# A four-layer stack on one core: rotary partners side by side, norms in tiles of 64 tokens, and another written order

## The chip, the core and the metric

The kernel runs on one core of a Trainium2 chip. The metric is the time of one execution on the device in microseconds, as the median over runs. A core has five engines that work side by side, each through its own queue of instructions in order: TensorE (matrix products, PE in the profile, its weight loads PEld), VectorE (DVE), ScalarE (ACT), GpSimd (POOL) and SyncE (SP), which issues nearly all transfers here. Products land in PSUM, a small memory of 8 banks that TensorE alone fills and that VectorE and ScalarE empty. All else lies in SBUF, 128 partitions of one row each.

## What is computed

The input is 16 sequences of 256 tokens with 128 features. Four blocks follow one another: causal attention with 16 small heads; a feed-forward part with a choice of two experts in eight; a retention layer; and at last a stack of six layers, each with local attention and a feed-forward part. The change lies in the stack's attention. Cut to what matters:

```python
def attn_layer(x, Wqkv, qs, ksc, Wo):          # 16 heads of 64, windows of 32
    q, k, v = heads(x @ Wqkv)
    q, k = l2norm(q) * qs, l2norm(k) * ksc
    q = q * cos * scale + rotate_half(q) * sin * scale
    k = k * cos / scale + rotate_half(k) * sin / scale
    out = local_attention(q, k, v)             # own window and the one before, causal, softmax
    return out @ Wo
for i in range(6):
    x = attn_layer(shift_tokens(x), ...) + x
    x = ffn_layer(shift_tokens(x), ...) + x
```

`rotate_half` exchanges the two halves of a head's 64 features and turns one's sign: feature f and feature f + 32 are rotary partners. All is in float32.

## The kernel before

**Units.** In the stack the kernel works with features on partitions and tokens along the row. A unit is one sequence in one layer's attention; 6 layers by 16 sequences give 96 units, two of them (a pair of sequences) sharing one feed-forward part. A unit has four head groups G. Two partition halves by two slots (`hf`) make four heads of 64 features in each group; q and k are the index k. The methods of `Unit` are its steps, named in the order by short words:

- `pqk` (L925): projection of group G, q or k, into one PSUM bank; two banks take turns (`ps_qk`). `sq` (L933, ScalarE), `t2` (L942) and `rot` (L947, both VectorE) read it: the squares, the product with the sines and the product with the cosines, the last one into the tile `qk`, of which there are eight (two units).
- `sw` (L958, SP): the partners' products change places, by transfers from `t` to `t2s`. `add` (L964, GpSimd) adds them to `qk`.
- `nr` (L973): sums of squares of each head and token, by products with `gather`, a matrix of zeros and ones that also sets the row in which each sum lands. 8 tiles of 32 tokens by 2 slots by 4 groups, in two words `nr.0` and `nr.1`. `rnA` (L985), `rnB` (L988), `rnC` (L991): max, square root, reciprocal.
- `bcW` (L997) sends the reciprocals to DRAM (`ndr`, two in turn), `bcR` (L1006) reads those of a group back, spread over 64 partitions at a time, into `bc` (one tile for each group). `norm` (L1013, GpSimd) multiplies `qk` by them.
- `s` (L1042): scores, in PSUM tiles shared with `o` (two in turn). `sm`, `mx`, `sub`, `exp`, `su`, `rec`, `nm`, `tp` (L1058 to L1098): band, maximum, subtraction (GpSimd), exponential (ScalarE), sum, reciprocal, multiplication (GpSimd), transposition, for each slot `hu`.
- `xt`, `xc` (L1021, L1029): the tokens transposed as values. `o` (L1112), `oTc` (L1125), `y` (L1131), `xsu` (L1141): weighted sums, their copy, the output product (value and output weights multiplied ahead), and the residual.
- `fn` to `xsf` (L1157 to L1261) in `Forward`: the feed-forward part of a pair.

`nr`, `xt`, `y` and the feed-forward products share two PSUM banks in turn (`ps_m`).

**Order.** `ORDER` (L1278) is written out by hand or by a planner beforehand: a list of words `step.arguments:distance`. One round of the loop runs the whole list once for two units; the distance says which unit a word belongs to, counted from the round's first. So words of a dozen units, early projections and late feed-forward steps, alternate, and each engine's queue is what the list has for it. Nothing is reordered later. `BRIDGE`, another such list, leads from the retention layer into the stack; `FIRST` orders the blocks before it.

Of the kernel before, what the change touches and what calls it, by code (L numbers as in the profile page):

```python
# [28 lines left out]
DEPTH, H2, D2, WIN = 6, 16, 64, 32  # L29
INNER = H2 * D2  # L30
# [8 lines left out]
def _tables():  # L39

    c = {}
    c["ident"] = np.eye(P)
    i = np.arange(P)
    diag = np.where(i[None, :] > i[:, None], NEG, 0.0)
    c["mask0"] = np.concatenate([diag, np.zeros((P, P)), diag], 1)

    qi = i[:, None] % WIN  # L50
    key = np.arange(WIN)[None, :]
    band = np.concatenate([key >= qi, key <= qi], 1)
    first = band & ((i[:, None] >= WIN) | (np.arange(2 * WIN)[None, :] >= WIN))
    band = np.where(np.stack([first, band], 1), 0.0, NEG)
    c["band"] = np.repeat(band[:, :, None, :], 4, 2).reshape(P, 512)


    t = np.arange(T, dtype=np.float64)
    inv = 1.0 / 10000.0 ** (np.arange(0, DK1, 2) / DK1)
    f = np.outer(t, inv)  # L60
    cs = np.concatenate([np.cos(f), np.cos(f)], 1)
    sn = np.concatenate([-np.sin(f), np.sin(f)], 1)
# [12 lines left out]

    half = np.arange(0, D2, 2, dtype=np.float64)
    f = (1.0 / 10000.0 ** (half / D2))[:, None] * t[None, :]
    base = (half + 0.4 * D2) / (1.4 * D2)  # L80
    sc = base[:, None] ** ((t - T // 2) / (WIN // 2))[None, :]
    both = np.stack([8.0 * sc, 1.0 / sc])
    cos = np.stack([np.cos(f) * both, np.cos(f) * both], 1)
    sin = np.stack([np.sin(f) * both, -np.sin(f) * both], 1)
    tabs = np.stack([cos, sin]).transpose(2, 3, 0, 1, 4).reshape(D2, -1)
    c["rot2"] = np.tile(tabs, (2, 1))


    e = np.arange(WIN)
    sb = np.arange(16)  # L90
    gather = (i[:, None, None] // D2 == e[None, None, :] // 16) & (e[None, None, :] % 16 == sb[None, :, None])
    c["gather"] = gather.reshape(P, -1)


    e = np.arange(NE)
    sel = (np.arange(NE * RANK)[None, :] // RANK) == e[:, None]
    c["expand"] = np.concatenate([sel, np.zeros((P - NE, NE * RANK))])
    before = (e[None, :] < e[:, None]).astype(np.float64).reshape(1, -1)
    c["before"] = np.broadcast_to(before, (P, NE * NE))
    return {k: np.ascontiguousarray(v, dtype=np.float32) for k, v in c.items()}  # L100
# [7 lines left out]
def kernel(ctx: ExitStack, tc: tile.TileContext, a: dict, widths: dict, out: bass.AP):  # L108
    nc = tc.nc
# [6 lines left out]
    dram = ctx.enter_context(tc.tile_pool(name="dram", bufs=1, space=bass.MemoryType.DRAM))  # L116
# [13 lines left out]
    c = {}  # L130
# [576 lines left out]
    for g in range(NPAIR):  # L707
        xt = xres.tile([P, 2, XW], F32, name=f"xs{g}")
# [84 lines left out]
    for n in range(2):  # L793
        t = ea.tile([P, 2, 4, 4, 32], F32, name=f"less{n}")
# [49 lines left out]
    s2 = ctx.enter_context(tc.tile_pool(name="s2", bufs=2, **right))  # L844
# [5 lines left out]
    for n in range(NRING):  # L850
        t = lw.tile([P, 2, 2, WIN + T], F32, name=f"qk{n}")
        nc.gpsimd.memset(t[:, :, :, 0:WIN], 0.0)
        ring.append(t)
    band = c["band"]
    gather = c["gather"].rearrange("p (s b m) -> p s b m", s=2, b=8)

    ndr = [dram.tile([2, H2, T], F32, name=f"ndr{n}") for n in range(2)]
    def load_qk(l, G):

        w = lw.tile([P, 2, 2, P], F32, tag=f"wqk{G}", name=f"wqk{l}_{G}")  # L860
        src = a["wqk2"][l].rearrange("d (g k h n) -> d g k h n", g=4, k=2, h=2)
        nc.sync.dma_start(out=w, in_=src[:, G])
        return w
# [40 lines left out]
    class Unit:  # L904
# [48 lines left out]

        def sw(self, G):

            for to in range(4):
                at = to ^ 1
                nc.sync.dma_start(  # L958
                    out=self.t_2s(G)[32 * to : 32 * to + 32], in_=self.t_2(G)[32 * at : 32 * at + 32]
                )  # L960

        def add(self, G):
            to = self.qk_t[G][:, :, :, WIN : WIN + T]
# [2 lines left out]


        def nr(self, part):
            nr = self.misc("nr")[:, 0:64]
            for b in range(4 * part, 4 * part + 4):  # L970
                for slot in range(2):
                    for G in range(4):
                        nc.tensor.matmul(  # L973
                            nr[32 * G : 32 * G + 32, :],
                            lhsT=gather[:, slot, b, :],
                            rhs=self.squares(G)[:, :, slot, WIN * b : WIN * b + WIN],
                            start=(b == 0 and slot == 0),
                            stop=(b == 7 and slot == 1),
                        )

        def r_n(self):
            return self.tile(s2, [P, 64], "rn")

        def rnA(self):
            nc.vector.tensor_scalar(self.r_n(), self.misc("nr")[:, 0:64], 1e-24, None, ALU.max)  # L985

        def rnB(self):
            nc.scalar.activation(self.r_n(), self.r_n(), AF.Sqrt)  # L988
# [2 lines left out]
            nc.vector.reciprocal(self.r_n(), self.r_n())  # L991

        def bcast(self, G):
            return self.tile(s2, [P, 2, 2, T], "bc", G, tag=f"bc{G}", bufs=1)

        def bcW(self):
            nc.sync.dma_start(  # L997
                out=ndr[self.u % 2].rearrange("k h (b t) -> (h b) k t", t=WIN),
                in_=self.r_n().rearrange("p (k t) -> p k t", k=2),
            )  # L1000

        def bcR(self, G):

            for r in range(2):
                at = 4 * G + 2 * r
                nc.sync.dma_start(  # L1006
                    out=self.bcast(G)[64 * r : 64 * r + 64].rearrange("p k s t -> p k (s t)"),
                    in_=ndr[self.u % 2][:, at : at + 2].rearrange("k s t -> k (s t)").partition_broadcast(64),
                )

        def norm(self, G):
            to = self.qk_t[G][:, :, :, WIN : WIN + T]
            nc.gpsimd.tensor_tensor(to, to, self.bcast(G), ALU.mult)  # L1013


        def xt(self):
# [126 lines left out]
    class Forward(Unit):  # L1143
# [132 lines left out]


    ORDER = """  # L1278
        rnB:0 rs:-4 rot.3.1:0 t2.1.1:1 pqk.1.0:1 fg.2:-6 oTc.1.0:-2 sq.1.0:1 s.1.1.1:-1 sw.3:0 s.1.0.0:-1 rnC:0
        s.1.1.0:-1 t2.1.0:1 s.1.0.1:-1 oTc.1.1:-2 y.0:-2 bcW:0 sq.1.1:1 rot.1.0:1 rot.1.1:1 pqk.0.1:1 sw.1:1 y.1:-2  # L1280
        pqk.0.0:1 sm.1:-1 exp.0:-1 mx.1:-1 y.2:-2 t2.0.1:1 add.3:0 su.0:-1 rot.0.1:1 z:-4 sq.0.1:1 sub.1:-1 sq.0.0:1
        exp.1:-1 t2.0.0:1 rot.0.0:1 pqk.3.1:1 bcR.2:0 add.1:1 bcR.0:0 rec.0:-1 pqk.3.0:1 y.3:-2 sq.3.0:1 nm.0:-1
        su.1:-1 rec.1:-1 bcR.1:0 sq.3.1:1 rot.3.1:1 t2.3.1:1 nm.1:-1 bcR.3:0 norm.0:0 t2.3.0:1 sw.0:1 gl.2:-6 pqk.2.0:1
        rot.3.0:1 sq.2.0:1 pqk.2.1:1 fa.2:-6 tp.0:-1 xsu:-2 tp.1:-1 add.0:1 sq.2.1:1 nr.0:1 o.1:-1 nr.1:1 fh.2:-6
        trf:-4 oTc.1.0:-1 norm.1:0 rot.2.1:1 oTc.1.1:-1 norm.3:0 rot.2.0:1 t2.2.1:1 t2.2.0:1 pqk.1.1:2 rnA:1 xt:0 rnB:1
        rnC:1 sw.3:1 fz:-4 sw.2:1 o.0:-1 pqk.1.0:2 bcW:1 oTc.0.0:-1 norm.2:0 xc:0 bcR.3:1 fg.0:-4 s.0.1.0:0 add.3:1
        sq.1.1:2 t2.1.0:2 s.0.0.0:0 sq.1.0:2 s.0.0.1:0 oTc.0.1:-1 gl.0:-4 s.0.1.1:0 sm.0:0 fy:-6 bcR.2:1 fa.0:-4 mx.0:0
        t2.1.1:2 s.1.1.1:0 add.2:1 s.1.0.1:0 s.1.0.0:0 xsf:-6 s.1.1.0:0 sub.0:0 rot.1.1:2 sm.1:0 y.0:-1 pqk.0.0:2
        y.1:-1 mx.1:0 rot.1.0:2 pqk.0.1:2 exp.0:0 t2.0.0:2 rot.0.0:2 su.0:0 sq.0.0:2 norm.3:1 t2.0.1:2 sq.0.1:2
        pqk.2.1:2 bcR.0:1 norm.2:1 sub.1:0 sw.1:2 rot.0.1:2 exp.1:0 y.2:-1 bcR.1:1 sq.2.1:2 rec.0:0 fh.0:-4 pqk.2.0:2  # L1290
        y.3:-1 sw.0:2 rot.2.1:2 t2.2.1:2 pqk.3.0:2 fg.1:-4 s.0.0.1:1 norm.0:1 sq.2.0:2 su.1:0 norm.1:1 rec.1:0 gl.1:-4
        s.0.1.1:1 s.0.1.0:1 nm.0:0 rot.2.0:2 xsu:-1 s.0.0.0:1 t2.2.0:2 nm.1:0 fn:-2 tp.0:0 sm.0:1 pqk.3.1:2 nat:-2 xt:1
        tp.1:0 fa.1:-4 t2.3.0:2 xc:1 sq.3.1:2 o.0:0 sq.3.0:2 oTc.0.0:0 add.1:2 mx.0:1 t2.3.1:2 nr.0:2 rot.3.0:2 sw.2:2
        oTc.0.1:0 add.0:2 pqk.1.1:3 st:-2 add.2:2 fh.1:-4 sub.0:1 nr.1:2 o.1:0 rnA:2
    """.split()


# [156 lines left out]
```

## Time and profile before

| what | value |
| --- | --- |
| median of 3 runs | 3719.79 us (3716.75 to 3724.08) |
| the profiled execution's own time | 3729.29 us |
| its span, from first to last instruction | 3727.5 us |
| TensorE busy | 3369.8 us (90%) |
| GpSimd busy | 2855.7 us (77%) |
| VectorE busy | 2656.2 us (71%) |
| ScalarE busy | 2021.2 us (54%) |
| transfers | 459.58 MB, mean 123 GB/s |
| swap transfers (`t2s<-t`) | 1536 of 128 KB |
| norm reads (`bc<-ndr`) | 768 of 256 KB |

The profile comes from one execution. Its page gives each engine's busy time, the same in 40 equal slices of the span, the chain of work that ended last (followed back from the end, at each step to what released it), and groups of equal instructions with their mean time and the idle time of the engine ahead of them. A wait is written as "engine tile line <- what ended it", with the total, the number of times and the longest. SPq is SP's queue, busy while it issues a transfer. A matrix product in float32 leaves two records. Views of the trace show the same for any stretch of time.

### The profile page before, as it was taken

What the parts mean: (1) busy time and instruction counts of PE and PEld (TensorE: products, weight loads), DVE (VectorE), ACT (ScalarE), POOL (GpSimd) and SP (SyncE); (2) the same over time, 40 slices, a digit from 0 to 9 for tenths busy, and PEclk for the clock granted to TensorE, in tenths of its full rate; (3) what the DMA queues carried; (4) which work ended last, traced back from release to release, by engine and by line L of the source; (5) the groups of instructions that cost most, each with busy time, mean ns of one, the idle gap of its engine ahead of it and who ended that gap; (6) DMA issues with size and microseconds to landing.
All of it is one profiled execution on the core that took longest, in us unless ns stands there. A gap on an engine that the chain in (4) does not pass through costs nothing.

```text
span 3727.5 us, 124065 instructions
## 1 busy us (share of the span) xinstructions
PE 3369.8 (90%) x53280; PEld 2360.1 (63%) x53280; DVE 2656.2 (71%) x5196; ACT 2021.2 (54%) x2933; POOL 2855.7 (77%) x1753
## 2 busy tenths in 40 slices
PE   5999986699999999999999999999999999999997
PEld 3666665466666666666666666666666666666664
DVE  4667664577777777777786777777777777777773
ACT  2455543355656555556555565555565655555552
POOL 2445445688888888888888888888988898888882
PEclk7999998799999999999999999999999999999999
DMA  3111103566665656565656666656566666656561
GB/s 94 27 38 33 41 15 95 132 145 149 136 156 121 161 137 158 124 158 123 166 128 148 140 139 143 151 134 153 134 143 150 143 140 152 136 135 143 130 150 31
DMA packets 245698, 459.58 MB, mean 123 GB/s; under 512 B 66462, under 2 KB 85020, under 8 KB 245020
## 3 DMA queue, kind: packets, MB, share of 16 engines
q1 hardware_dynamic: 244716, 451.38, 52.0%
q8 instruction: 419, 6.86, 0.9%
q14 instruction: 131, 1.07, 0.1%
q10 hardware_dynamic: 432, 0.26, 0.0%
HBM read 235.47 MB, written 14.68 MB: 67 GB/s over the span
## 4 chain that ended last, share of the span: by engine, by line
PE 29%; DMA 20%; DVE 17%; POOL 14%; SPq 9%; issue 7%; ACT 3%; POOLq 0%; DVEq 0%; ACTq 0%
DMA t2s<-t 10%; DMA bc<-ndr 7%; SPq L958 5%; PE o L1112 5%; POOL qk L964 5%; POOL qk L1013 5%; PE pqk L925 4%; DVE t L942 4%; SPq L1006 4%; DVE qk L947 3%; DVE pT L1098 3%; PE s L1042 2%; PE nr L973 2%; PE p L327 2%; PE fy L1246 2%
## 5 line engine op out<-in xcount | busy, mean ns | idle before, releaser
L964 POOL TENSOR_TENSOR qk<-qk,t2s 128x1024 f32<-128x1024 f32 x384 | 904.5, 2367 | 305.1 <-DMA t2s<-t 272.8
L925 PE MATMUL pqk<-xs,wqk 128*128 128x256 f32 x3072 | 831.6, 394 | 107.2 <-DVE t L942 44.5
L1013 POOL TENSOR_TENSOR qk<-qk,bc 128x1024 f32<-128x1024 f32 x384 | 899.7, 2364 | 34.1 <-DMA bc<-ndr 26.7
L933 ACT ACTIVATE sq<-pqk 128x512 f32<-128x512 f32 x768 | 445.2, 600 | 588.9 <-DVE qk L947 310.9
L925 PEld LDWEIGHTS pqk<-xs,wqk 128*128 128x128 f32 x3072 | 554.6, 192 | 320.1 <-PE pqk L925 64.8
L942 DVE TENSOR_TENSOR t<-pqk,rot 128x512 f32<-128x512 f32 x768 | 515.5, 682 | 334.4 <-PE pqk L925 145.8
L1131 PE MATMUL y<-oT,m 128*128 128x256 f32 x3072 | 739.3, 384 | 11.6 <-issue 7.6
L1131 PEld LDWEIGHTS y<-oT,m 128*128 128x128 f32 x3072 | 577.9, 191 | 97.6 <-issue 9.6
L947 DVE TENSOR_TENSOR qk<-pqk,rot 128x512 f32<-128x512 f32 x768 | 514.7, 680 | 152.8 <-ACT sq L933 77.0
L1125 ACT COPY oT<-o 128x1024 f32<-128x1024 f32 x384 | 380.7, 1018 | 356.1 <-PE o L1112 356.1
L1073 POOL TENSOR_TENSOR sm<-sm,mx 128x1024 f32<-128x1024 f32 x192 | 365.7, 1905 | 87.5 <-DVE mx L1069 72.2
L1112 PE MATMUL o<-pT,xv 32*128 32x512 f32 x3072 | 395.0, 627 | 33.7 <-DVE pT L1098 28.4
L1042 PEld LDWEIGHTS s<-qk 64*32 64x32 f32 x24576 | 265.1, 105 | 218.2 <-POOL qk L1013 69.1
L1091 POOL TENSOR_TENSOR sm<-sm,rec 128x1024 f32<-128x1024 f32 x192 | 361.7, 1904 | 33.8 <-DVE rec L1087 33.3
L1042 PE MATMUL s<-qk 64*32 64x64 f32 x24576 | 309.4, 226 | 61.1 <-POOL qk L1013 41.6
L1058 DVE TENSOR_TENSOR sm<-s,c_band 128x1024 f32<-128x1024 f32 x192 | 234.2, 1220 | 151.6 <-PE s L1042 146.4
L973 PEld LDWEIGHTS nr<-sq,c_band 128*32 128x32 f32 x12288 | 185.2, 111 | 160.5 <-issue 93.4
L1077 ACT ACTIVATE sm<-sm 128x1024 f32<-128x1024 f32 x192 | 202.8, 1056 | 153.1 <-POOL sm L1073 149.2
L1112 PEld LDWEIGHTS o<-pT,xv 32*128 32x128 f32 x3072 | 142.3, 188 | 185.3 <-issue 100.3
L1098 DVE STREAM_TRANSPOSE pT<-sm 128x1024 f32<-128x1024 f32 x192 | 237.6, 1237 | 19.1 <-POOL sm L1091 17.6
L1222 ACT ACT_TABLE_LOAD x138 | 177.1, 1283 | 133.1 <-PE fg L1216 125.4
L973 PE MATMUL nr<-sq,c_band 128*32 128x64 f32 x12288 | 220.1, 222 | 30.2 <-issue 29.0
(191 smaller groups left out, 4444.1 us busy)
## 6 DMA issues: line engine op xcount, KB each, us to landing
t2s<-t SPq DMA_DIRECT2D x1536, 128.0 KB
bc<-ndr SPq DMA_DIRECT2D x768, 256.0 KB
wqk<-in_wqk_dram SPq DMA_DIRECT2D x24, 256.0 KB
rot_l<-in_rot_dram SPq DMA_DIRECT2D x12, 256.0 KB
rot<-rot_l SPq DMA_DIRECT2D x12, 256.0 KB
rot<-rot SPq DMA_DIRECT2D x6, 512.0 KB
ndr<-rn SPq DMA_DIRECT2D x96, 32.0 KB
wv<-in_wv_dram SPq DMA_DIRECT2D x6, 512.0 KB
```

What stands on the lines that cost most here:

```text
L925: nc.tensor.matmul(self.p_qk(G, k)[:, hf, :], lhsT=weights["qk", G, self.l][:, k, hf, :], rhs=xq, start=True, stop=True)
L933: nc.scalar.activation(self.squares(G)[:, k], self.p_qk(G, k), AF.Square)
L942: nc.vector.tensor_tensor(self.t_2(G)[:, k], self.p_qk(G, k), self.turn(1, k), ALU.mult)
L947: nc.vector.tensor_tensor(self.qk_t[G][:, k, :, WIN : WIN + T], self.p_qk(G, k), self.turn(0, k), ALU.mult)
L964: nc.gpsimd.tensor_tensor(to, to, self.t_2s(G), ALU.add)
L973: nc.tensor.matmul(nr[32 * G : 32 * G + 32, :], lhsT=gather[:, slot, b, :], rhs=self.squares(G)[:, :, slot, WIN * b : WIN * b + WIN], star ...
L1013: nc.gpsimd.tensor_tensor(to, to, self.bcast(G), ALU.mult)
L1042: nc.tensor.matmul(ps[32 * b : 32 * b + 32, r2, tt, G // 2, G % 2, :], lhsT=qk[G][rows, 0, hu, WIN + at : 2 * WIN + at], rhs=qk[G][rows, 1 ...
L1073: nc.gpsimd.tensor_tensor(s3, s3, self.t_mx(hu)[:, :, None].to_broadcast([P, 16, 2 * WIN]), ALU.subtract)
L1112: nc.tensor.matmul(self.p_o(tt, b // 2)[:, b % 2].rearrange("f (h g) q -> f h g q", g=4), lhsT=self.t_xv()[rows, n, tt, :], rhs=pT[rows, : ...
L1125: nc.scalar.copy(self.t_oT()[:, :, at : at + 2 * WIN].rearrange("f h (b q) -> f b h q", b=2), self.p_o(tt, c))
L1131: nc.tensor.matmul(self.misc("y")[:, 0:T], lhsT=weights["m", self.l][:, h, :], rhs=self.t_oT()[:, h, :], start=(h == 0), stop=(h == H2 - 1),)
```

## The change

Three things are changed in the stack.

1. **Rotary partners on neighbouring partitions.** The columns of the projection weights are permuted on the host, and the cosine, sine and scale tables with them, so that features f and f + 32 of a head lie on partitions 2f and 2f + 1 of its half. The swap then exchanges even and odd partitions: two transfers of 64 rows, each taking every second partition, where there were four of 32 neighbouring rows.
2. **Norms in tiles of 64 tokens.** `gather` has 8 row patterns for each half where it had 16, a product of `nr` has 128 columns (q and k by 64 tokens) where it had 64, and there are half as many. The norm tile is 128 x 128. It is written to DRAM as it stands, and a read takes 8 rows in one run of 4 KB for each partition. `bc` now has its elements ordered slot, token tile, q or k, token, and `norm` reads it through a rearranged pattern.
3. **`ORDER` is written anew**: the same 203 words, at other places and, for many, other distances. `BRIDGE` and `FIRST` are as before.

```diff
-    tabs = np.stack([cos, sin]).transpose(2, 3, 0, 1, 4).reshape(D2, -1)
+    tabs = np.stack([cos, sin]).transpose(3, 2, 0, 1, 4).reshape(D2, -1)
...
-    sb = np.arange(16)
-    gather = (i[:, None, None] // D2 == e[None, None, :] // 16) & (e[None, None, :] % 16 == sb[None, :, None])
+    sb = np.arange(8)
+    gather = (i[:, None, None] // D2 == e[None, None, :] // 8) & (e[None, None, :] % 8 == sb[None, :, None])
...
-    ndr = [dram.tile([2, H2, T], F32, name=f"ndr{n}") for n in range(2)]
+    ndr = [dram.tile([P, P], F32, name=f"ndr{n}") for n in range(2)]
...
-            for to in range(4):
-                at = to ^ 1
-                nc.sync.dma_start(
-                    out=self.t_2s(G)[32 * to : 32 * to + 32], in_=self.t_2(G)[32 * at : 32 * at + 32]
-                )
+            for to in range(2):
+                nc.sync.dma_start(out=self.t_2s(G)[to:P:2], in_=self.t_2(G)[1 - to : P : 2])
...
-            nr = self.misc("nr")[:, 0:64]
-            for b in range(4 * part, 4 * part + 4):
+            nr = self.misc("nr")[:, 0:P]
+            for b in range(2 * part, 2 * part + 2):
...
-                            rhs=self.squares(G)[:, :, slot, WIN * b : WIN * b + WIN],
+                            rhs=self.squares(G)[:, :, slot, 64 * b : 64 * b + 64],
...
-            return self.tile(s2, [P, 2, 2, T], "bc", G, tag=f"bc{G}", bufs=1)
+            return self.tile(s2, [P, 2, 4, 2, 64], "bc", G, tag=f"bc{G}", bufs=1)
...
-            nc.sync.dma_start(
-                out=ndr[self.u % 2].rearrange("k h (b t) -> (h b) k t", t=WIN),
-                in_=self.r_n().rearrange("p (k t) -> p k t", k=2),
-            )
+            nc.sync.dma_start(out=ndr[self.u % 2], in_=self.r_n())
...
-                at = 4 * G + 2 * r
+                at = 32 * G + 8 * r
                 nc.sync.dma_start(
-                    out=self.bcast(G)[64 * r : 64 * r + 64].rearrange("p k s t -> p k (s t)"),
-                    in_=ndr[self.u % 2][:, at : at + 2].rearrange("k s t -> k (s t)").partition_broadcast(64),
+                    out=self.bcast(G)[64 * r : 64 * r + 64].rearrange("p s b k t -> p (s b k t)"),
+                    in_=ndr[self.u % 2][at : at + 8].rearrange("e x -> (e x)").partition_broadcast(64),
                 )
...
-            nc.gpsimd.tensor_tensor(to, to, self.bcast(G), ALU.mult)
+            to = to.rearrange("p k s (b t) -> p k s b t", t=64)
+            nc.gpsimd.tensor_tensor(to, to, self.bcast(G).rearrange("p s b k t -> p k s b t"), ALU.mult)
```

The places of the old order that the prediction works with, and of the new one:

```diff
-        pqk.0.0:1 sm.1:-1 exp.0:-1 mx.1:-1 y.2:-2 t2.0.1:1 add.3:0 su.0:-1 rot.0.1:1 z:-4 sq.0.1:1 sub.1:-1 sq.0.0:1
-        exp.1:-1 t2.0.0:1 rot.0.0:1 pqk.3.1:1 bcR.2:0 add.1:1 bcR.0:0 rec.0:-1 pqk.3.0:1 y.3:-2 sq.3.0:1 nm.0:-1
...
+        nm.1:0 tp.1:0 y.2:-1 sq.2.0:2 pqk.2.1:2 bcR.0:1 sq.2.1:2 t2.2.0:2 y.3:-1 o.0:0 xsf:-6 t2.2.1:2 oTc.0.0:0 nr.0:2
+        nr.1:2 rnA:2 oTc.0.1:0 bcR.2:1 add.0:2 xsu:-1 o.1:0 norm.0:1 bcR.1:1 rnB:2 bcR.3:1 norm.1:1 fg.2:-4 oTc.1.0:0
+        sw.3:2 gl.2:-4 sw.2:2 fa.2:-4 norm.2:1 s.0.1.0:1 norm.3:1 oTc.1.1:0 s.0.1.1:1 rot.2.1:2 s.0.0.0:1 rot.2.0:2
+        s.0.0.1:1 rnC:2 add.2:2 fh.2:-4 bcW:2 xt:2 pqk.1.1:3 pqk.2.0:3 bcR.0:2 fg.0:-4 sm.0:1 mx.0:1 bcR.2:2 s.1.0.0:1
+        t2.2.0:3 s.1.1.0:1 t2.1.1:3 rot.1.1:3 add.3:2 s.1.0.1:1 bcR.3:2 sq.2.0:3 s.1.1.1:1 sq.1.1:3 sm.1:1 rot.2.0:3
+        xc:2 y.0:0 bcR.1:2 mx.1:1 sub.0:1 gl.0:-4 exp.0:1 pqk.2.1:3 sq.2.1:3 pqk.1.0:3 y.1:0 su.0:1 rec.0:1 sub.1:1
+        rot.2.1:3 xt:1 nm.0:1 y.2:0 t2.2.1:3 rot.1.0:3 exp.1:1 su.1:1 rec.1:1 xc:1 pqk.0.0:3 t2.1.0:3 nm.1:1 tp.0:1
+        sw.2:3 tp.1:1 norm.0:2 rot.0.0:3 sq.1.0:3 t2.0.0:3 y.3:0 norm.1:2 pqk.0.1:3 o.0:1 xsu:0 sq.0.0:3 sq.0.1:3
...
-    wqk2 = qkv[:, :, : 2 * INNER].reshape(DEPTH, D, 2, 4, 4 * D2).transpose(0, 1, 3, 2, 4)
+    wqk2 = qkv[:, :, : 2 * INNER].reshape(DEPTH, D, 2, 4, 4, 2, WIN).transpose(0, 1, 3, 2, 4, 6, 5)
...
-    qks = np.stack([f["L1_ffn_q_scale"], f["L1_ffn_k_scale"]]).transpose(2, 1, 0).reshape(D2, -1)
+    qks = np.stack([f["L1_ffn_q_scale"], f["L1_ffn_k_scale"]]).reshape(2, DEPTH, 2, WIN)
+    qks = qks.transpose(3, 2, 1, 0).reshape(D2, -1)
```

More of the change, by code (lines that the diff above doesn't have):

```diff
@@ L854 @@
     band = c["band"]
-    gather = c["gather"].rearrange("p (s b m) -> p s b m", s=2, b=8)
-    ndr = [dram.tile([2, H2, T], F32, name=f"ndr{n}") for n in range(2)]
+    gather = c["gather"].rearrange("p (s b m) -> p s b m", s=2, b=4)
+    ndr = [dram.tile([P, P], F32, name=f"ndr{n}") for n in range(2)]
     def load_qk(l, G):
@@ L975, in nr @@
                             lhsT=gather[:, slot, b, :],
-                            rhs=self.squares(G)[:, :, slot, WIN * b : WIN * b + WIN],
+                            rhs=self.squares(G)[:, :, slot, 64 * b : 64 * b + 64],
                             start=(b == 0 and slot == 0),
-                            stop=(b == 7 and slot == 1),
+                            stop=(b == 3 and slot == 1),
                         )
         def r_n(self):
-            return self.tile(s2, [P, 64], "rn")
+            return self.tile(s2, [P, P], "rn")
         def rnA(self):
-            nc.vector.tensor_scalar(self.r_n(), self.misc("nr")[:, 0:64], 1e-24, None, ALU.max)
+            nc.vector.tensor_scalar(self.r_n(), self.misc("nr")[:, 0:P], 1e-24, None, ALU.max)
         def rnB(self):
@@ L1278 @@
     ORDER = """
-        rnB:0 rs:-4 rot.3.1:0 t2.1.1:1 pqk.1.0:1 fg.2:-6 oTc.1.0:-2 sq.1.0:1 s.1.1.1:-1 sw.3:0 s.1.0.0:-1 rnC:0
-        s.1.1.0:-1 t2.1.0:1 s.1.0.1:-1 oTc.1.1:-2 y.0:-2 bcW:0 sq.1.1:1 rot.1.0:1 rot.1.1:1 pqk.0.1:1 sw.1:1 y.1:-2
-        pqk.0.0:1 sm.1:-1 exp.0:-1 mx.1:-1 y.2:-2 t2.0.1:1 add.3:0 su.0:-1 rot.0.1:1 z:-4 sq.0.1:1 sub.1:-1 sq.0.0:1
-        exp.1:-1 t2.0.0:1 rot.0.0:1 pqk.3.1:1 bcR.2:0 add.1:1 bcR.0:0 rec.0:-1 pqk.3.0:1 y.3:-2 sq.3.0:1 nm.0:-1
-        su.1:-1 rec.1:-1 bcR.1:0 sq.3.1:1 rot.3.1:1 t2.3.1:1 nm.1:-1 bcR.3:0 norm.0:0 t2.3.0:1 sw.0:1 gl.2:-6 pqk.2.0:1
@@ L1284 @@
[L1284 to L1293, printed above, removed]
@@ L1294 @@
-        oTc.0.1:0 add.0:2 pqk.1.1:3 st:-2 add.2:2 fh.1:-4 sub.0:1 nr.1:2 o.1:0 rnA:2
+        s.1.0.0:0 rot.3.0:1 fh.0:-6 add.1:1 st:-4 s.1.1.0:0 rot.1.0:2 t2.3.0:1 norm.2:0 norm.3:0 nr.1:1 rnA:1 fg.1:-6
+        pqk.1.1:2 sq.1.1:2 fa.1:-6 sw.0:1 s.0.0.1:0 sq.1.0:2 rot.1.1:2 s.0.1.1:0 t2.1.1:2 sw.3:1 s.1.1.1:0 t2.1.0:2
+        rnB:1 s.1.0.1:0 pqk.0.0:2 sm.0:0 sm.1:0 pqk.0.1:2 rs:-4 o.1:-1 gl.1:-6 sq.0.0:2 add.0:1 t2.0.0:2 fh.1:-6
+        rot.0.0:2 add.3:1 sq.0.1:2 mx.0:0 sw.1:2 rnC:1 mx.1:0 t2.0.1:2 sub.0:0 sub.1:0 pqk.3.1:2 z:-4 rot.3.1:2
@@ new lines @@
+        oTc.1.0:-1 add.1:2 oTc.1.1:-1 trf:-4 fz:-4 exp.0:0 t2.3.1:2 rot.0.1:2 su.0:0 fy:-6 rec.0:0 exp.1:0 y.0:-1
+        su.1:0 pqk.3.0:2 nm.0:0 rot.3.0:2 sq.3.0:2 y.1:-1 rec.1:0 sq.3.1:2 tp.0:0 bcW:1 t2.3.0:2 sw.0:2 pqk.2.0:2
+        nm.1:0 tp.1:0 y.2:-1 sq.2.0:2 pqk.2.1:2 bcR.0:1 sq.2.1:2 t2.2.0:2 y.3:-1 o.0:0 xsf:-6 t2.2.1:2 oTc.0.0:0 nr.0:2
+        nr.1:2 rnA:2 oTc.0.1:0 bcR.2:1 add.0:2 xsu:-1 o.1:0 norm.0:1 bcR.1:1 rnB:2 bcR.3:1 norm.1:1 fg.2:-4 oTc.1.0:0
+        sw.3:2 gl.2:-4 sw.2:2 fa.2:-4 norm.2:1 s.0.1.0:1 norm.3:1 oTc.1.1:0 s.0.1.1:1 rot.2.1:2 s.0.0.0:1 rot.2.0:2
@@ L1295 @@
+        pqk.3.1:3 oTc.0.0:1 fn:-2 s.0.0.0:2 s.0.1.0:2 t2.0.1:3 rot.0.1:3 pqk.3.0:3 sw.1:3 add.2:3 nat:-2 oTc.0.1:1
+        t2.3.1:3 fa.0:-4 sq.3.1:3 sq.3.0:3 rot.3.1:3 pqk.1.0:4 nr.0:3
     """.split()
```

## The prediction, made before the changed kernel ran

> **What bounds the kernel now.** I read the page's busy shares and slices first. They show two parts: a first stage of some 590 us, and then a steady loop, in which TensorE is busy in nearly every slice and GpSimd in 80 to 90% of it.
>
> ```profile
> PE 3369.8 (90%) x53280; PEld 2360.1 (63%) x53280; DVE 2656.2 (71%) x5196; ACT 2021.2 (54%) x2933; POOL 2855.7 (77%) x1753
> ...
> PE   5999986699999999999999999999999999999997
> ...
> POOL 2445445688888888888888888888988898888882
> ```
>
> The length of a unit (one sequence in one layer; there are 96) comes from the rows of the norm tile: its first step starts 96 times between 594.6 and 3623.9 us, so a unit takes 3029.3/95 = 31.9 us and a round of the loop (two units) 63.8 us. Then the busy times of 800 to 3500 us, 42.3 rounds of nothing but loop:
>
> ```profile
> L985 DVE TENSOR_SCALAR rn<-nr x96: 213/225/226, 594.6 to 3623.9; 128x64 f32<-128x64 f32 x96
> ```
>
> ```profile
> 800.00:3500.00 2700.00, 2521.32 (x42779) 1766.36 (x42775) 2026.50 (x3136) 1556.01 (x2082) 2315.25 (x1204) 0.99 0.62 143
> ```
>
> In order: TensorE 93.4%, its weight loads, VectorE 75%, ScalarE 58%, GpSimd 86%, clock 0.99, DMA 62%. TensorE idles 178.7 us there, 4.2 us a round. No other engine is nearer to full, so the loop is bound by TensorE's work (59.6 us a round) plus these 4.2 us. The waits of TensorE in the same stretch say whose they are:
>
> ```profile
> PE pqk L925 <- DVE t L942: 38.9, 45, 1.6
> PE s L1042 <- POOL qk L1013: 27.6, 28, 2.4
> PE nr L973 <- issue: 26.9, 18, 3.2
> PE pqk L925 <- DVE qk L947: 19.1, 43, 0.8
> PE o L1112 <- DVE pT L1098: 15.6, 37, 2.1
> PE pqk L925 <- ACT sq L933: 13.7, 37, 0.5
> ```
>
> The largest is a projection that waits for VectorE to empty its PSUM bank; 45 times in 42 rounds is one fixed place of the written order. The chain that ended last shows why such waits come about: transfers and their issue hold a good part of it.
>
> ```profile
> PE 29%; DMA 20%; DVE 17%; POOL 14%; SPq 9%; issue 7%; ACT 3%; POOLq 0%; DVEq 0%; ACTq 0%
> DMA t2s<-t 10%; DMA bc<-ndr 7%; SPq L958 5%; PE o L1112 5%; POOL qk L964 5%; POOL qk L1013 5%; PE pqk L925 4%; DVE t L942 4%; SPq L1006 4%; DVE qk L947 3%; DVE pT L1098 3%; PE s L1042 2%; PE nr L973 2%; PE p L327 2%; PE fy L1246 2%
> ```
>
> The chain can't shrink by what these rows hold, since TensorE's own work stands just behind it: no change can gain more than the 4.2 us a round (48 rounds, 202 us) plus what it takes off TensorE.
>
> [...] The timeline decides: projections, y steps and feed-forward products start one after the other at a fixed spacing (0.86, 1.73, 0.95 us) with no gap.
>
> **Part 1: norm sums in tiles of 64 tokens (nr).** A unit's 64 products of 64 columns become 32 of 128 columns; the columns streamed stay the same. On the timeline 64 records of nr take 1.03 us (16.1 ns each), 2.06 us a unit. A projection's 4 records of 256 columns take 0.865 us, 0.845 ns a column. Four column groups run side by side, so 64 columns cost at least 13.5 ns a record: 2.6 ns is left over per record. With 128 columns: 27.0 + 2.6 = 29.6 ns x 64 records = 1.90 us; with the surplus in proportion (the o rows take 120.5 ns for 512 columns on four row groups, 11% above 108), 30 ns, 1.92 us. Ends: no gain at all, or 1.03 us if a record cost the same whatever its width. I take 0.2 us x 96 = **19 us off TensorE**.
>
> The tile behind it is twice as wide: max 225 ns, square root 257 ns, reciprocal 552 ns now. A reciprocal of 16 elements takes 248 ns (rec), so 6.3 ns an element, and 128 take 0.96 us. The other two lie between unchanged and doubled. The path from nr to the sent norms grows by 0.4 to 0.9 us. It is hidden: between nr and the first s of the unit the new order keeps 26 and 30 us of TensorE's work (before: 29 and 27), and the path needs some 14 (max 0.3, table load and root 1.6, reciprocal 1.0, write 0.4 and the 1.4 that SP waits for it, reads 1.2 and 5.9 to land, multiply 2.4). Uncovered it would cost at most 0.9 us x 96 = 86 us.
>
> **Part 2: the swap (sw).** 16 transfers of 32 rows a unit become 8 of 64 rows, same bytes. One issue holds the SP queue for 0.588 us, so four hold it 2.4 us; a transfer of 64 rows (bc, L1006) 0.607 us, two 1.2 us. SP is freed of 4 x 1.2 = 4.8 us a unit, and all queued behind a swap goes out sooner. From the first issue of a swap to the add that waited for it the shortest seen is 4.25 us: 2.4 of issue, 1.85 of landing. What a 4 KB packet will take is the open price: the trace has 159 ns in transfers over all 128 partitions, and a median of 293 ns in the swaps over 32. An engine has 4 packets of each new transfer: 0.64 to 1.17 us (now 2 packets, 0.59). The shortest swap comes to 3.1 to 3.6 us, 0.65 to 1.15 less. I take the slow end, since rows of the swap are nearest to it.
>
> [...]
>
> GpSimd waits for swaps now (239.9 us in 84 waits in the stretch, 5.7 us a round). With 1.2 us of issue gone from each swap these shrink, GpSimd being the next fullest engine. TensorE feels it only through s (27.6 us); what is late next is part 4.
>
> **Part 3: norms sent (bcW, bcR, norm).** The write has 128 rows of 512 B for 256 of 128 B. The reads move the same bytes in 4 KB rows: two 2 KB packets now take 0.168 us at best and 0.28 typically, a 4 KB one 0.159 to 0.293. So nothing, either way. The multiply (2364 ns) reads the norms in runs of 64: unchanged if runs cost nothing (the subtraction L1073 goes over runs of 64 in 1905 ns), up to 2.53 us by the first stage's add of two full operands (1266 ns for 512). 8 x 0.17 = 1.4 us a round at most, within GpSimd's 9.1 us of idle. Value: nothing.
>
> **Part 4: the order.** No instruction is added, each engine's queue is permuted. I compared the orders at every reuse of a PSUM buffer: TensorE's work between the buffer's last write and its rewrite, against what the releasing engine has in its queue over the same words. Before, projection pqk.3.0 of the odd unit: TensorE has y.2 and one projection (1.73 + 0.87 = 2.6 us), VectorE sm, mx, su (3.6) and four rotary multiplies (2.7), 6.3 us: 3.7 short. This is the kind of wait that heads the list. Summed over a round the old order is short by 17.4 us (projections 10.6 in eight places; nr and xt behind y and nr 5.7; s and o 1.1). The new one: 7.4 (projections 2.2 in three places and 3.0 behind ScalarE's sq.3.1, after two exps; s and o 2.1; the mixed banks none). At the old ratio, 4.2 us of idle for 17.4, the new idle is 1.8 us, a gain of 2.4. But waits for data are not in this sum, and one gets tighter: o.0 of the odd unit comes after 10.9 us of TensorE's work behind its scores, before 14.0, while its softmax needs 1.22 + 1.22 + 1.91 + 1.28 + 1.06 + 1.20 + 0.25 + 1.90 + 1.24 = 11.3 us (sm, mx, sub, table load, exp, su, rec, nm, tp). So I take half: **1.2 us x 48 = 58 us**. One ScalarE table load a round also goes (seven switches become six, 1.28 us); ScalarE has idle time, so nothing.
>
> **Sum.** -19 - 58 = -77 us on the profiled execution's 3729.3 us (span 3727.5): 3652. The median of the runs is 9.5 us lower, so the forecast against it is **3643 us**. The first stage and the 104 us of tail are left as they are: their order is unchanged, and in the tail no words compete.
>
> **Rivals.**
> 1. The swap wasn't the bound and the order gains nothing: only part 1 counts, 3720 - 19 = 3701; with nothing from it, 3720, within 0.2% (all I could tell from no change). For it: GpSimd's idle hid the swaps. Against: the projection's fixed shortfall goes.
> 2. Slower: the odd unit's softmax becomes the bound. Its sub and nm stand in GpSimd's queue behind add.2 and add.3 of the next unit, which wait for swaps. One such wait is now 239.9/84 = 2.9 us; if it falls there each round, o.0 is 11.3 + 2.9 - 10.9 = 3.3 us late. It decides above 1.6 us a round (1.2 + 0.4 gained). 48 x (3.3 - 1.6) = +82: 3802.
> 3. All shortfalls go as summed, and the faster packets clear the rest: idle falls to 1.2 us a round, 48 x 3.0 + 19 = -163: 3557.
> 4. The interleaved rows don't speed the landing at all and only issue time goes: half of part 4, 3672; within the forecast's own range.
>
> **Chances.** Forecast 3600 to 3690 (rival 4 in it): 0.52; rival 3 below 3600: 0.11; rival 1, 3690 to 3712: 0.12 and 3712 to 3727: 0.07; rival 2: 0.18. Faster 0.75, same 0.07, slower 0.18. The range for 8 in 10 runs from 3585 to 3785.
>
> **What would show it.** Right: nr near 0.95 us per half (32 records each); SP's issues of t2s near 0.6 us and half as many; 4 KB packets between 159 and 293 ns; TensorE's idle near 3 us a round; pqk waits for VectorE well below 58 us in the stretch. Wrong: o waiting for pT every round for 2 us and more; s waiting for norms; a norm multiply over 2.5 us (GpSimd then sets the pace at 64 us a round from about 3.5 us each: 9.1/8 on top of 2.36).

## The result, and the profile after

The changed kernel takes 3760.35 us (median of 4 runs, 3754.58 to 3766.81), against 3721.93 us of the kernel before in runs on the same chip (3716.75 to 3728.07). The ratio is 1.0103 with a 95% interval of 1.0078 to 1.0128: slower by 1.0%, where 2% faster was forecast. The profiled execution took 3754.58 us, its span is 3752.9 us.

I read the same views as before: the page's busy shares, slices and chain, then the steady stretch of 800 to 3500 us.

```profile
PE 3364.8 (90%) x47136; PEld 2376.2 (63%) x47136; DVE 2687.2 (72%) x5196; ACT 1960.4 (52%) x2887; POOL 2857.5 (76%) x1753
...
PE   5899986899989999899999899998999989997887
...
POOL 2445445789888889887888788988898888886772
...
PE 56%; DVE 18%; ACT 13%; issue 6%; POOL 4%; DMA 3%; SPq 1%; DVEq 0%; POOLq 0%; ACTq 0%
```

TensorE is busy 5 us less in all, and the chain that ended last has lost its transfers: DMA went from 20% to 3% of it, SP's issue from 9% to 1%. But the last slices of TensorE, which were 9 each, are now 7 8 8, and GpSimd's are 6 7 7. The time was not lost evenly.

The busy times of the stretch (same columns as before: TensorE, its weight loads, VectorE, ScalarE, GpSimd, clock, DMA share, GB/s), then what TensorE waited for in it (total, times, longest):

```profile
800.00:3500.00 2700.00, 2504.68 (x37203) 1772.78 (x37201) 2040.32 (x3115) 1486.57 (x2022) 2301.74 (x1193) 0.99 0.49 143
```

```profile
PE pqk L925 <- ACT sq L933: 47.3, 42, 1.2
PE y L1126 <- ACT xv L1024: 45.9, 39, 1.4
PE pqk L925 <- issue: 31.4, 7, 6.3
PE pqk L925 <- DVE qk L947: 24.4, 73, 0.5
PE s L1037 <- issue: 17.3, 17, 2.4
PE s L1037 <- POOL qk L1008: 17.1, 6, 5.2
```

The list has changed hands. The wait that headed it before (a projection behind VectorE's `t`, 38.9 us) is nearly gone, but two new ones come once in each of the 42 rounds, and two more are rare and long: 7 waits of up to 6.3 us, 6 of up to 5.2.

To find where they lie, I cut the execution into rounds, at the starts of the residual addition `xsu` of every second unit on VectorE, and grouped the rounds: those inside a layer, the two at each of the five layer ends, and the last five of all. Times in us:

| run (profiled) | up to the first round | 32 inside layers (median of one) | 10 at layer ends (mean of one) | last 5 (mean of one) | after them | span |
| --- | --- | --- | --- | --- | --- | --- |
| before | 721.4 | 1984.3 (61.6) | 651.3 (65.1) | 314.3 (62.9) | 56.2 | 3727.5 |
| after | 711.9 | 1958.0 (61.0) | 671.4 (67.1) | 356.2 (71.3) | 55.3 | 3752.9 |
| after minus before | -9.5 | -26.3 | +20.1 | +41.9 | -0.9 | +25.4 |

Inside the layers the change gains. It loses 62.0 us in 15 rounds: those in which one layer gives way to the next, and the last five.

**The last rounds.** SP's issues in the last layer (start, duration, in us from the span's start), then VectorE's sum, GpSimd and TensorE over the same stretch. `x2` counts merged instructions, and square brackets hold the idle time ahead and what ended it:

```profile
3511.43 1.25 SPq L1000 DMA_DIRECT2D bc<-ndr  x2
3524.98 0.40 SPq L1269 DMA_DIRECT2D out_dram<-f_res  x1
3525.42 4.12 SPq L1000 DMA_DIRECT2D bc<-ndr  x6
```

```profile
3524.27 0.69 DVE L1268 TENSOR_TENSOR f_res<-f_res,tr_e 128x512 f32<-128x512 f32 x1 [3.34 <-PE tr_e L140]
```

```profile
3533.56 6.94 POOL L1008 TENSOR_TENSOR qk<-qk,bc 128x1024 f32<-128x1024 f32 x3 [11.28 <-DMA bc<-ndr]
```

```profile
3535.95 0.47 PE L1037 MATMUL s<-qk 64*32 64x64 f32 x16 [4.91 <-POOL qk L1008]
3538.25 0.47 PE L1037 MATMUL s<-qk 64*32 64x64 f32 x16 [1.83 <-POOL qk L1008]
3540.55 1.41 PE L1037 MATMUL s<-qk 64*32 64x64 f32 x80 [1.83 <-POOL qk L1008]
```

SP reads the norms of one group (two issues) and then issues nothing for 12.3 us. The next instruction in its queue is the store of a finished result (L1269), which the word `xsf` issues in the last layer only and which waits for VectorE's sum, done at 3524.96 us. The six norm reads of the next three groups stand behind it and go out the moment it has. GpSimd's multiplication waits 11.28 us for them, and TensorE's scores 4.91 + 1.83 + 1.83 = 8.6 us for GpSimd. Each of the last five rounds has such a wait (TensorE's longest in it takes 4.5 to 6.0 us); they take 71.3 us on average.

**The layer ends.** SP, VectorE and TensorE at the first of them:

```profile
1066.78 1.14 SPq L957 DMA_DIRECT2D t2s<-t  x2
1072.23 5.61 SPq L862 DMA_DIRECT2D wqk<-in_wqk_dram  x2
1077.94 2.40 SPq L957 DMA_DIRECT2D t2s<-t  x4
```

```profile
1082.28 0.69 DVE L942 TENSOR_TENSOR t<-pqk,rot 128x512 f32<-128x512 f32 x1 [6.55 <-DMA t2s<-t]
```

```profile
1076.35 1.13 PE L925 MATMUL pqk<-xs,wqk 128*128 128x256 f32 x4
1077.31 1.02 PE L1224 MATMUL fa<-f_zT,w 128*128 128x512 f32 x2
...
1084.43 2.05 PE L925 MATMUL pqk<-xs,wqk 128*128 128x256 f32 x4 [6.09 <-issue]
```

Same pattern, other transfer. When the last sequence of a layer has made its projection of a group, the kernel issues the next layer's weights for it (L862) into the tile that the projection has just read. The two issues shown are those of two groups, and each waits for the last product of its own group's projection. SP issues nothing from 1067.9 to 1072.2 us, and within the 5.61 us nothing between the two, until the projection that starts at 1076.35 is done. Two swaps stand behind them; VectorE needs their buffer and waits 6.55 us, and TensorE waits 6.09 us for a projection's bank that VectorE empties only after that (the row calls it "issue").

### The profile page after: what moved, and what is told of

Same layout as the page of the kernel before. It is cut to its first block, busy times and chain, and to the rows that moved or that the text cites. A ratio compares the mean times of both kernels' runs of the same rounds, so it can differ in the third digit from the quotient of the medians.

```text
span 3752.9 us, 110221 instructions
## 1 busy us (share of the span) xinstructions
PE 3364.8 (90%) x47136; PEld 2376.2 (63%) x47136; DVE 2687.2 (72%) x5196; ACT 1960.4 (52%) x2887; POOL 2857.5 (76%) x1753
## 4 chain that ended last, share of the span: by engine, by line
PE 56%; DVE 18%; ACT 13%; issue 6%; POOL 4%; DMA 3%; SPq 1%; DVEq 0%; POOLq 0%; ACTq 0%
PE pqk L925 13%; PE y L1126 12%; PE o L1107 7%; PE nr L970 5%; DVE qk L947 5%; PE s L1037 4%; ACT sq L933 4%; PE fg L1211 3%; DVE su L1076 3%; DVE mx L1064 3%; DVE t L942 3%; PE p L327 2%; ACT L1217 2%; ACT L985 2%; POOL qk L1008 1%
## 5 line engine op out<-in xcount | busy, mean ns | idle before, releaser
L933 ACT ACTIVATE sq<-pqk 128x512 f32<-128x512 f32 x768 | 434.3, 598 | 1095.5 <-PE pqk L925 480.0
L1008 POOL TENSOR_TENSOR qk<-qk,bc 128x1024 f32<-128x1024 f32 x384 | 897.7, 2366 | 60.3 <-DMA bc<-ndr 60.3
L925 PE MATMUL pqk<-xs,wqk 128*128 128x256 f32 x3072 | 814.2, 396 | 140.1 <-ACT sq L933 61.5
L925 PEld LDWEIGHTS pqk<-xs,wqk 128*128 128x128 f32 x3072 | 566.9, 194 | 368.3 <-ACT sq L933 118.7
L1107 PE MATMUL o<-pT,xv 32*128 32x512 f32 x3072 | 427.6, 616 | 7.9 <-DVE pT L1093 6.5
L1107 PEld LDWEIGHTS o<-pT,xv 32*128 32x128 f32 x3072 | 175.1, 185 | 159.1 <-issue 89.2
L1076 DVE TENSOR_REDUCE su<-sm 128x16 f32<-128x1024 f32 x192 | 230.4, 1200 | 48.7 <-ACT sm L1072 48.5
L291 DVE CUSTOM_DVE_ANT_0 a_junk<-s,w_mask 128x128 f32<-128x128 f32 (+1 forms) x512 | 181.8, 355 | 76.7 <-PE s L279 63.6
L1064 DVE TENSOR_REDUCE mx<-sm 128x16 f32<-128x1024 f32 x192 | 230.2, 1199 | 1.7
```

The costliest lines, as they stand in the source:

```text
L925: nc.tensor.matmul(self.p_qk(G, k)[:, hf, :], lhsT=weights["qk", G, self.l][:, k, hf, :], rhs=xq, start=True, stop=True)
L933: nc.scalar.activation(self.squares(G)[:, k], self.p_qk(G, k), AF.Square)
L1008: nc.gpsimd.tensor_tensor(to, to, self.bcast(G).rearrange("p s b k t -> p k s b t"), ALU.mult)
L1107: nc.tensor.matmul(self.p_o(tt, b // 2)[:, b % 2].rearrange("f (h g) q -> f h g q", g=4), lhsT=self.t_xv()[rows, n, tt, :], rhs=pT[rows, : ...
```

## The experiments

All ratios are against runs of the kernel before on the same chip. The theory after this reading: the new transfers gained what was forecast or more, and the new order lost more than that, because some of its words carry a transfer that waits at the head of SP's queue with urgent transfers behind it. Its rivals: the new transfers themselves cost time; or the new order is slower in every round. Each experiment stands with what was expected of it before it ran.

**Each part by itself.** `e1_order_alone` is the kernel before with the new `ORDER`; `e2_old_order` is the changed kernel with the old one.

> The new order with the old swaps (four of 32 rows) and the old norms. Theory A (the new order has cheap rounds, and loses where a once-a-layer transfer waits at the head of the SP queue): rounds inside a layer get longer than the 60.8 us of the changed kernel, since the swaps are slower and SP is fuller; 3780 to 3830 us. Theory C (the order itself costs the 1%, transfers do not matter): 3760 to 3780 us, rounds of about 61.2.

> The new swaps and norms in the old order. Theory A: these parts gain by themselves, nr 0.2 us a unit and the swaps' waits on top: 3660 to 3700 us, GpSimd's waits for swaps well below 273 us. Theory C (swaps were hidden): 3700 us, only nr's 19 us.

Measured: e1 1.0436 [1.0392, 1.0480], median 3890.14 us; e2 0.9771 [0.9746, 0.9796], median 3650.46 us. Both lie outside what was expected: e1 above both of its theories, e2 somewhat below. So the new transfers with the old order gain 2.3%, and the new order takes that away and 1% more, 101 us of span between e2 and after. By the rounds: -5.5 up to the first, +22.9 inside layers, +27.3 at layer ends, +57.5 in the last five, -1.2 after them. The theory can explain the 84.8 us of the special rounds. The 22.9 us inside the layers are the last rival's: with the same transfers the new order is slower there than the old one. With the old transfers the new order does worst of all, also inside layers (62.8 us a round against 61.6). The waits of TensorE in e1 and in e2 in the stretch of 800 to 3500 us:

```profile
PE s L1042 <- issue: 61.0, 40, 3.9
...
PE nr L973 <- issue: 39.9, 31, 2.7
```

```profile
PE pqk L925 <- DVE t L942: 39.1, 45, 1.2
PE o L1107 <- DVE pT L1093: 24.8, 38, 2.1
PE pqk L925 <- DVE qk L947: 18.4, 44, 0.8
PE s L1037 <- POOL qk L1008: 13.4, 9, 2.4
```

The new order with the old swaps waits for scores and norm sums nearly every round (40 and 31 times); with the new swaps these waits are 17.3 and 1.7 us. e2 still has the projection's fixed wait of the old order, so its gain came from elsewhere: its scores wait 13.4 us for GpSimd, where the kernel before waited 27.6, and the norm sums' 26.9 us behind issue are gone from the list. Against e2, the waits of after name the cause inside the layers: its projections wait 25.4 us for VectorE where e2's wait 57.5, but TensorE waits 93.2 us for ScalarE (47.3 and 45.9) where e2 has 12.8.

**The store moved, the weight loads moved, both.** The store becomes a word of its own behind the norm reads; the loads go out after the next swap.

```diff
+        def res(self):
+            if self.last:
+                nc.sync.dma_start(out=out_tok[self.g], in_=self.t_res())
...
-        ... bcR.3:1 norm.1:1 ...
+        ... bcR.3:1 res:-6 norm.1:1 ...
```

```diff
-                weights["qk", args[0], l + 1] = load_qk(l + 1, args[0])
+                late.append((l + 1, args[0]))
...
+                    if method == "sw":
+                        while late:
+                            m, G = late.pop(0)
+                            weights["qk", G, m] = load_qk(m, G)
```

> The changed kernel, with the store of the last layer's result issued after bcR.3 of the running unit, not ahead of bcR.2, bcR.1 and bcR.3. Theory A: the last layer's rounds of 73 us fall to 62 to 65, in all 40 us less: 3715 to 3730 us. Theory B (the last feed-forward's transposes and additions on TensorE and VectorE cost the time): rounds stay at 72 or more, 3750 to 3765 us.

> The changed kernel, with the next layer's projection weights loaded behind the next swap instead of ahead of it. Theory A: TensorE's wait of 6 us at each of five layer ends goes, with the low clock after it: 5 x 6 to 9 us, 3715 to 3730 us. Theory B2 (the projection waits for the weights themselves): the wait stays or grows, 3755 to 3775 us.

> The changed kernel with both the result's store and the projection weights' loads moved behind the transfers that units in flight wait for. The two alone gave ratios to before of 0.9917 and 0.9963, against 1.0103 for the changed kernel: if they add up, 1.0103 - 0.0186 - 0.0140 = 0.978, 3640 to 3655 us. If they share one cause (a late unit that stays late), less: 0.985 to 0.992.

| run | ratio to before [95%] | median, us | 32 inside layers | 10 at layer ends | last 5 |
| --- | --- | --- | --- | --- | --- |
| e3, store | 0.9917 [0.9893, 0.9941] | 3704.32 | 1959.7 | 672.1 | 300.7 |
| e4, loads | 0.9963 [0.9947, 0.9979] | 3719.71 | 1959.4 | 632.2 | 356.2 |
| e5, both | 0.9837 [0.9811, 0.9863] | 3659.74 | 1950.7 | 632.1 | 299.8 |

Each edit moves only the rounds that it was made for: the store takes 55.5 us off the last five and nothing off the layer ends, the loads 39.2 us off the layer ends and nothing off the last five. e3 gained more than was expected (3704 us against 3715 to 3730), and e5 lies between its two theories: the ratios do not quite add up. Together the two moves undo the loss against the kernel before, which e5 beats by 1.6%. The old order with the new transfers and neither move (e2, 0.9771) is still ahead of it. In e3, SP's queue in the last layer, and in e4, SP's and TensorE's at a layer end:

```profile
3431.62 5.08 SPq L1000 DMA_DIRECT2D bc<-ndr  x8
3445.17 0.40 SPq L1272 DMA_DIRECT2D out_dram<-f_res  x1
```

```profile
1072.28 1.11 SPq L957 DMA_DIRECT2D t2s<-t  x2
1075.17 5.61 SPq L862 DMA_DIRECT2D wqk<-in_wqk_dram  x2
1080.95 1.11 SPq L957 DMA_DIRECT2D t2s<-t  x2
```

```profile
1081.43 1.10 PE L925 MATMUL pqk<-xs,wqk 128*128 128x256 f32 x4 [0.16 <-PE fa L1224]
```

In e3 all eight norm reads go out in one run, and the store waits behind them. In e4 the two loads take the same 5.61 us as before, so the second waits as long; but the swap that VectorE needs is already out, and TensorE's idle time of 6.09 us has become 0.16. It was not the transfer that cost, it was its place in the queue.

**What is left inside the rounds, and a better version.** e5 still has the two waits that come once a round:

```profile
PE y L1126 <- ACT xv L1024: 49.1, 41, 1.5
PE pqk L925 <- ACT sq L933: 48.4, 43, 1.2
```

Both are on ScalarE: `xc:2`, the copy that frees a shared bank for `y`, stands behind two squares, and `sq.3.1:2`, which frees a projection's bank, behind an exponential. `e6_new_order_mended` is e5 with these two words earlier; `e7_old_order_later` is e2 (the old order) with both transfers moved as in e5.

```diff
-        ... rec.0:0 exp.1:0 y.0:-1 ... rec.1:0 sq.3.1:2 tp.0:0 ...
+        ... rec.0:0 sq.3.1:2 exp.1:0 y.0:-1 ... rec.1:0 tp.0:0 ...
...
-        ... bcR.3:2 sq.2.0:3 s.1.1.1:1 sq.1.1:3 sm.1:1 rot.2.0:3 xc:2 y.0:0 ...
+        ... bcR.3:2 xc:2 sq.2.0:3 s.1.1.1:1 sq.1.1:3 sm.1:1 rot.2.0:3 y.0:0 ...
```

> The last kernel, with two words of the new order moved on ScalarE: xc ahead of the squares, and sq.3.1 ahead of the second exp. If TensorE is the bound in a round, its waits for ScalarE (48.3 us and 44.7 us in 42 rounds, 2.2 us a round) go and rounds fall from 60.8 to 58.6 us: ratio 0.95 to 0.965. If VectorE's or GpSimd's chain stands just behind, rounds stay at 60 to 60.8: 0.972 to 0.98.

> The old order with the new swaps and norms, and both kinds of transfer moved back likewise. Here the store and the loads stood behind most of what matters: TensorE waits at the layer ends for 1.6 us or so, and the last layer's rounds are 61 to 64 us. Expected: 0.970 to 0.977, little below the 0.977 without the move. If the theory of the SP queue is wrong and the moves help for another reason, 0.95 to 0.96 as in the new order.

Measured: e6 0.9685 [0.9669, 0.9701], median 3603.44 us, the fastest version of this study; e7 0.9726 [0.9706, 0.9746], 3618.38 us. e6 lies between its two theories, e7 within its first. In e6 both waits are gone, and a round inside a layer takes 59.8 us (median; e5 60.9). Inside the layers e5's 32 rounds take 1950.7 us in sum, e7's 1938.0 and e6's 1919.3. So with the two transfers moved and nothing else the new order is still behind the old one (0.9837 against 0.9726), and the two words on ScalarE put it ahead. Whether the old order would gain by such a search of its words was not tried. The old one had the same fault in smaller measure: against e2 (644.1 and 298.7 us) the moves take 27.6 us off its layer ends, but only 4.6 us off its last five rounds. What e6 waits for now:

```profile
PE pqk L925 <- DVE qk L947: 26.0, 76, 0.5
PE o L1107 <- DVE pT L1093: 24.7, 36, 1.1
```

The two words moved gave some 1.1 us a round of the 2.3 that the two waits had held: `o` waiting for its softmax, 0.2 us in the whole stretch of after, came up behind them with 24.7.

**The swap by itself, and which part of it.** `e8_swap_alone` is the kernel before with the new row order and swap only. `e9_four_interleaved` keeps e8's row order, but four transfers of 32 interleaved rows inside each half of the partitions. `e11_two_by_halves` has two transfers of 64 neighbouring rows, each half to itself: it leaves out the exchange of the partners, and keeps the bytes and the issues of e8.

```diff
             for to in range(2):
-                nc.sync.dma_start(out=self.t_2s(G)[to:P:2], in_=self.t_2(G)[1 - to : P : 2])      # e8
...
+            for r in range(2):                                                                     # e9
+                for to in range(2):
+                    at, end = 64 * r + to, 64 * r + 64
+                    nc.sync.dma_start(out=self.t_2s(G)[at:end:2], in_=self.t_2(G)[64 * r + 1 - to : end : 2])
...
+                rows = slice(64 * to, 64 * to + 64)                                                # e11
+                nc.sync.dma_start(out=self.t_2s(G)[rows], in_=self.t_2(G)[rows])
```

> The kernel before with the new swap alone (old norms, old order). If the swap carries the gain of the old order's 0.977, beyond nr's 19 us: 0.980 to 0.985. If the norms' 4 KB rows carry it: 0.99 to 1.0. GpSimd's waits for swaps, 273 us before and 96 us with all the new transfers, should be near 100 us in the first case.

> The new swap alone in the old order, but in four transfers again: even from odd and odd from even rows, first within partitions 0 to 63, then within 64 to 127. If it is the spread over all 128 partitions that makes a 4 KB packet cheap (164 ns at the median in the swap alone, 293 ns before), packets are back at 280 to 300 ns and the ratio to before is 0.997 to 1.003. If neighbouring rows make it cheap, packets stay near 165 ns and only the issue's time comes back: 0.992 to 0.996.

> The new swap alone in the old order, still two transfers of 64 rows, but each over one half of the partitions, rows to themselves: the exchange of partners is left out. It keeps the saved issues and gives up the spread. If the issues carry the swap's gain (0.9896), the ratio stays at 0.989 to 0.992. If the packets do, these are back at 280 to 300 ns, four of them in a row, and the ratio is 0.997 to 1.003.

| run | issues x rows, partitions spanned | ratio to before [95%] | 4 KB packet, median ns | GpSimd's waits for swaps, us |
| --- | --- | --- | --- | --- |
| before | 4 x 32, 32 | 1 | 293 | 272.8 |
| e9 | 4 x 32, 64 | 0.9994 [0.9975, 1.0013] | 293 | 236.4 |
| e11 | 2 x 64, 64 | 0.9921 [0.9904, 0.9938] | 281 | 205.3 |
| e8 | 2 x 64, 128 | 0.9896 [0.9875, 0.9918] | 164 | 106.9 |

The packets' times are medians of the trace's records of 4 KB packets from 800 to 3500 us, nearly all of them of swaps. The last column is a row of the swap tile's view in each run (us, times), over the whole span; in e8 it reads:

```profile
  DMA t2s<-t: 106.9, 72
```

In these four the median packet is fast only where one transfer's rows span all 128 partitions (164 ns); within half of them it stays at 281 to 293, interleaved or not. With the fast packets GpSimd's waits halve (205.3 to 106.9 us). In time, the larger share came with the halved issues (e9 to e11); the intervals of e11 and e8 overlap, so what the span adds to the time, some 0.25%, is not settled. The swap as a whole gave less than the 1.5 to 2% expected if it carried e2's gain. Why a packet is faster over all 128 partitions, no run shows.

**The norms by themselves.** `e10_norms_alone` is the kernel before with point 2 of the change only: old swap, old order.

```diff
-            for b in range(4 * part, 4 * part + 4):
+            for b in range(2 * part, 2 * part + 2):
...
-                    in_=ndr[self.u % 2][:, at : at + 2].rearrange("k s t -> k (s t)").partition_broadcast(64),
+                    in_=ndr[self.u % 2][at : at + 8].rearrange("e x -> (e x)").partition_broadcast(64),
```

> The new norms alone (tiles of 64 tokens, 4 KB rows), with the old swap and the old order. If the parts add up, 0.9771 / 0.9896 = 0.987: nr's 0.13 to 0.3 us a unit (12 to 28 us) and some 20 us from shorter waits. If the norms gain by nr alone: 0.993 to 0.996.

Measured: 0.9885 [0.9855, 0.9915], median 3675.74 us, some 43 us. The norm products' rows are busy 210.4 us in all where they were 220.1, some 10 us. The other 33 are shorter waits; which of the halved products, the single write or the 4 KB reads shortens them was not tried apart, and stays open. Multiplied, e8 and e10 give 0.978, and e2, which has both, 0.977: the two add up, each with about half.

## Why the prediction was wrong, point by point

**Right: the products.** The norm products' rows are busy 220.1 us before and 204.3 us after, 0.16 us a unit less. The sum took 0.2, though its own working gave 0.14 to 0.16. The multiplication stayed at 2366 ns. The reciprocal on the wider tile was put at 0.96 us and took 0.943, the max between unchanged and doubled (291 ns for 225), and no wait of a score is put down to them:

```profile
L988 DVE RECIPROCAL rn<-rn x96: 939/943/954, 590.6 to 3651.6; 128x128 f32<-128x128 f32 x96
```

**Put at nothing: the transfers.** The sum gave the shorter swaps no term of their own, as they were to reach TensorE through part 4, and of the norms as sent it said "So nothing, either way". With the old order, products and transfers gain 2.3% (e2), 85 us of 3721.9: the swap alone 1.0% (e8), the norms alone 43 us, 33 of them beyond the products and from a source that stays open (e10). That 85 is near the sum's 77 for everything is luck: 58 of the 77 were to come from the order. For a packet I took the slow end, 293 ns, because the swaps' own rows were nearest; it was the fast end, 164 (e8). The shortest time from a swap's first issue to the add that waited for it is 3.0 us in e8, where 3.1 to 3.6 was worked out.

**Half right inside the rounds: the PSUM sum.** What it said of VectorE came true: projections waiting for it fell from 58 us to 25 in the stretch. What it said of ScalarE did not: TensorE's waits for it rose from 13.7 to 93.2 us. The sum had listed the first place (`sq.3.1` after two exponentials, 3.0 us short). Of the second, `y` behind `xc`, it said "the mixed banks none": I counted the work of each engine between a write and the rewrite, but not that ScalarE's squares ahead of `xc` themselves wait on VectorE (2.90 and 0.89 us ahead of the one at 1060.50 us of after). TensorE's idle time in a round inside layers fell from 4.2 to 3.7 us on average, where near 3 was forecast. The gain over 32 such rounds was 26.3 us where 1.6 a round (order and products) would be 51, and it is not the order's: the products and transfers gain 49.2 there by themselves (e2), and the order takes 22.9 of it back. With its two words on ScalarE moved and the two transfers too, 65.0 are gained (e6).

**The step that failed** is part 4's term, 1.2 us a round or 58 us for the new order. The order costs 101 us instead (e2 to after): 84.8 in the 15 special rounds, 22.9 inside the layers, and 6.7 less elsewhere. The larger part lies in the end of the sum: "The first stage and the 104 us of tail are left as they are: their order is unchanged, and in the tail no words compete." and, behind it, in part 4, which compared the orders "at every reuse of a PSUM buffer" and nowhere else. Two words carry a transfer in special rounds only: the projection of a layer's last sequence (next weights) and `xsf` in the last layer (the store). Part 4 moved both within SP's queue and I did not follow what they issue. In the new order six norm reads and two swaps stand directly behind them; the old one paid 4.6 and 27.6 us for these places (e2 to e7). e3 and e4 put their price at 55.5 and 39.2 us, measured by moving these transfers alone; the sum of the two is more than the 62.0 us by which these rounds grew, as the new transfers had gained 22.8 us there (before to e2). I had also taken every round for 1/48 of the gain, when 15 of them are of another kind: the stretch of 800 to 3500 us that I called "nothing but loop" holds all five layer ends. And the 63.8 us that I took for a round count from a norm tile that the bridge issues; cut at `xsu`, a round before is 62.0 us on average inside layers and 65.1 at their ends.

**The rivals.** The sign of the second rival came true and its mechanism did not: `o` waits for its softmax 6.5 us in the whole of after. Rival 1, an order that gains nothing, was nearer, but in none did the order itself cost time at SP or ScalarE. A rival that said "a queue blocked by a transfer that comes in special rounds only" was missing. Rival 4 (packets no faster) is excluded by 164 ns. Rival 3's floor, 3557, was not reached even by e6, in which `o` waits for its softmax again.

## What to carry to other kernels

When an order is rewritten, list every instruction that each word issues in its special rounds too (first, last, layer change), and for each transfer ask two things: what does it wait for, and what stands behind it in the same queue. A bulk transfer that must wait for a late producer belongs behind the urgent ones; moving two of them was worth 2.6% here (e5 against after), with no instruction added or removed. When a queue's work is counted against a wait, count also what its own entries wait for: two words on ScalarE were worth another 1.5% (e6 against e5). And measure a change of several parts against each part alone: here the transfers and products were 2.3% faster, and the new order was 3.4% slower on top of them and 4.4% slower by itself.

## What the runs showed of the hardware that was not expected

- A 4 KB packet between two on-chip tiles took 164 ns when its transfer took every second one of 128 partitions, and 293 ns when it took every second one of 64 (medians of e8 and e9). Interleaving alone (e9) left the median at the 293 ns of before.
- An idle time of 6 us cost TensorE more than itself here. The stretch behind the layer end shown above runs at a granted clock of 0.50 (the last column but two), 4 us of the stretch ahead of it at 1.00:

```profile
1074.00:1078.00 4.00, 4.00 (x82) 2.93 (x78) 1.29 (x2) 2.81 (x4) 3.75 (x2) 1.00 0.10 35
1084.40:1088.00 3.60, 3.57 (x36) 2.56 (x36) 2.64 (x10) 0.00 (x0) 3.60 (x3) 0.50 0.00 0
```

  So the four products of `pqk` after the wait take 2.05 us at 0.50, where they took 1.10 in e4 after 0.16 us of idle, and four products of `pqk` 1.13 at 1.00 in the first of these two stretches (1074.06 us). By the trace's clock records 6.8 us at each of the five layer ends of after are at 0.50. In e5, which has neither of the long waits, there is no such record between 690 and 3598 us, and the mean granted clock of 800 to 3500 us is 1.00 (0.99 in after). The kernel before has records of 3.4 us at 0.50 in its loop too, without any idle time of over 3.5 us there, so these runs do not tell how short a wait is enough.
